# A GRU over 128 steps: both first rows of x on ScalarE's queue, r's input weights in two halves at the head of SyncE's, ten products of zeros ahead of the first real ones

## The chip, the core and the metric

The kernel runs on one core of a Trainium2 chip. A core has TensorE (PE, matrix products; its weight loads are listed as PEld), VectorE (DVE), ScalarE (ACT), GpSimd (POOL) and SyncE (SP), which only issues transfers here. Data come from HBM over DMA transfers, which an engine's instruction stream issues and 16 DMA engines carry out. Operands lie in on-chip memory of 128 partitions; TensorE writes to accumulator banks (PSUM), from which the vector engines read.

The metric is the time of one execution on the device in microseconds, as the median of several runs. Lower is better.

## The reference

`x` has 64 sequences of 128 steps with 512 values, `cond` the first state of 64 x 512. Each step of the GRU is

```python
comb = concatenate([x_t, h])
z = sigmoid(comb @ Wz + bz)
r = sigmoid(comb @ Wr + br)
h_cand = tanh(concatenate([x_t, r * h]) @ Wh + bh)
h_new = (1 - z) * h + z * h_cand
h_next = tanh(h_new @ Wp + bp)   # every 4th step but the last; otherwise h_new
```

and the result is `x` plus the sequence of `h_new`. All is float32. The upper 512 rows of Wz, Wr and Wh act on x, the lower 512 on the state.

## The kernel before, in words

**Two parts of each product.** The parts of the gates that come from x do not depend on the state. They are made ahead of the recurrence, as units in a queue that fill TensorE between the state's products (`put`, `fill`). For steps 0 to 3 they are plain products; from step 4 on, groups of steps share block products by a fast scheme on TensorE whose sums run on GpSimd and VectorE. The state's products (`gate`, four products of K for each of two halves of the batch) write to the tiles `rec_0`, `rec_1` and `rec_z`. The order of all instructions on each engine is the order in which the program writes them (`manual_schedule`); nothing reorders it.

**Names.** `wx` holds the weights for x of the three gates, `[128, K=4, 3, 512]`, 4 bytes a value: 1 MB for each gate, of which the four K parts are 256 KB each. `wh` holds those for the state. `x_rows` (L138) holds steps 0 and 1 of x as 64 rows of 512 each, 128 KB a step; `xT` the turned x. `scratch_q`, `_r`, `_a`, `_x`, `_y` are accumulator banks.

**The start, in the order of the program.**

1. VectorE sets the tile `zeros` (L67), GpSimd makes the identity matrix `ident`.
2. L140-141: the two rows of x are issued, step 0 over SyncE's queue (SP), step 1 over ScalarE's (ACT).
3. L142-143: r's weights for x are issued over SP in three pieces: K part 0, K part 1, and K parts 2 and 3 together (`load_wx`, L126 and L127).
4. L144-145: the biases over GpSimd's queue. L147: a dummy sigmoid on ScalarE, which loads its function table.
5. L149-152: z's and h's weights over SP, each in two halves of 512 KB; then step 2 of x (`load_step`, L122). L154: GpSimd copies one value of r's last K part, and by that waits for it; then it issues the two loads of the first state (L156).
6. L689: `idle(28)`, 28 products of zeros on TensorE (L236). Each has 512 columns of bf16 and one of four groups of 32 output partitions; four in a row go to the four groups, and they turn through `rec_0`, `rec_1` and `rec_z`. Nothing reads what they write.
7. L690-691: `turn_rows` turns the rows of steps 0 and 1, four transposes each on TensorE (L306) and one copy to `xT` each on VectorE (L311).
8. L692: `split_bias` on VectorE (L205-210). L693: `idle(4)`, four more products of zeros.
9. L694-696: r's products with x for steps 0 and 1 (L246), in the order of the pieces of the weights: for a piece, all its K parts of step 0, then of step 1. One K part of one step is 4 products, which the trace lists as 8 matmuls.
10. Then the loads of the state's weights over SP (L697-701), the first two K parts of z's products, the spreading of the biases (L217), the rest of z, h's products, step 2's and 3's, and from L720 on the first state and the recurrence.

SP's transfers share eight counters in turn. From the ninth on, a transfer is issued when the one eight places ahead of it has landed.

Of the kernel before, what the change touches and what calls it, by code (L numbers as in the profile page):

```python
# [18 lines left out]
def kernel(  # L19
# [14 lines left out]
    nc = tc.nc  # L34
    B, T, D = x.shape
# [7 lines left out]
    K = D // P  # L43
# [52 lines left out]
    def part(q):  # L96
        return slice(q * V, (q + 1) * V)
# [15 lines left out]
    both_queues = (nc.sync, nc.scalar)  # L113
# [12 lines left out]
    def load_wx(i, k0, k1):  # L126
        nc.sync.dma_start(  # L127
            out=wx[:, k0:k1, i, :],
            in_=gates_in[i][:D].rearrange("(p k) n -> p k n", k=K)[:, k0:k1],
        )  # L130
# [6 lines left out]
    x_rows = one.tile([P, Q4, S, J], F32, tag="xs0", name="x_rows")[:B].rearrange(  # L137
        "b t h u -> b (t h u)"  # L138
    )
    for t in range(2):  # L140
        both_queues[t].dma_start(out=x_rows[:, ts(t, D)], in_=x[:, t, :])  # L141
    for k0, k1 in ((0, 1), (1, 2), (2, K)):  # L142
        load_wx(R, k0, k1)
    for i, b in enumerate((br, bh, bz)):  # L144
        nc.gpsimd.dma_start(out=bias_in[:, i, :], in_=b.rearrange("(q j) -> q j", q=NQ))
# [9 lines left out]
    for h in range(S):  # L155
        nc.gpsimd.dma_start(  # L156
            out=h_rows[:, h, :],
            in_=h0[ts(h, V), :].rearrange("b (q j) -> q b j", q=NQ),
# [44 lines left out]
    def split_bias():  # L203
        high, low = thirds[:NQ], thirds[2 * V : 2 * V + NQ]
        nc.vector.tensor_copy(high, bias_in)  # L205
        nc.vector.tensor_sub(rest, bias_in, high)
        nc.vector.tensor_copy(middle, rest)
        nc.vector.tensor_copy(thirds[V : V + NQ], middle)
        nc.vector.tensor_sub(rest, rest, middle)
        nc.vector.tensor_copy(low, rest)  # L210
# [23 lines left out]
    def idle(n):  # L234
        for i in range(n):
            nc.tensor.matmul(  # L236
                rec[i // NQ % 3].rearrange("p a d n -> p (a d n)")[part(i % NQ)],
                lhsT=zeros[:, :V],
                rhs=zeros,
                start=True,  # L240
                stop=True,
            )
# [441 lines left out]
    def now(units):  # L684
        put(units)
        both(len(units))
# [3 lines left out]
    turn_rows(0, scratch[4])  # L690
    turn_rows(1, scratch[3])
    split_bias()  # L692
    idle(4)  # L693
    for part_k in (slice(0, 1), slice(1, 2), slice(2, K)):  # L694
        for t in range(2):
            now(first[R][t][part_k])
    load_wh(R)  # L697
# [373 lines left out]
```

## Time and profile before

| | |
|---|---|
| median of 3 runs | 1259.13 us (1259.06 to 1259.54) |
| the profiled execution's own time | 1258.66 us |
| its span, first to last instruction | 1256.6 us |
| TensorE busy | 1248.4 us |
| ScalarE, VectorE, GpSimd busy | 836.3, 809.1, 909.7 us |
| bytes moved, mean rate | 61.09 MB, 49 GB/s |

How to read the rows that follow. In an order of time, a row is: start in us from the span's start, length in us, engine, line, operation, out<-in, shape, count; in brackets the engine's idle time before it and what ended it. Like instructions in a row are merged. A "q" behind an engine's name (SPq, ACTq) means its instruction stream, which issues transfers. Matmuls are pipelined and their ends are modelled, so the distance from one start to the next tells more than the length. In a table of stretches, a row is: from:to, length, the busy time of PE, PEld, DVE, ACT and POOL with the number of instructions, the TensorE clock listed, the share of the 16 DMA engines and GB/s. In a DMA row, the last number is the time from issue to landing (the median, if there are several). In the list of waits: total, times, longest.

### The profile page before, as it was taken

The page shows a single profiled execution, that of the slowest core. Times are in us where ns is not written, and L with a number is a line of the kernel's source. Part 1 is how long each engine was busy: PE and PEld are TensorE (multiplying, and loading weights), DVE is VectorE, ACT ScalarE, POOL GpSimd, SP SyncE. Part 2 cuts the span into 40 slices and gives each one's busy share as a digit, 9 for nine tenths or more (in the row PEclk, how much of TensorE's full clock was granted, in tenths as well). Part 3 has the DMA queues.
Part 4 walks back from the last instruction along what each step waited for, and adds up shares of the span by engine and source line. Part 5 has one row for each costly group of instructions (what it writes and reads, how often), then busy time and mean ns, then how long its engine had stood idle before and what let it go on. Part 6 is the DMA issues. An engine that isn't in the chain of part 4 may idle for free.

```text
span 1256.6 us, 60732 instructions
## 1 busy us (share of the span) xinstructions
PE 1248.4 (99%) x25952; PEld 1155.6 (92%) x25952; DVE 809.1 (64%) x2183; ACT 836.3 (67%) x2687; POOL 909.7 (72%) x1032
## 2 busy tenths in 40 slices
PE   9999999999999999999999999999999999999998
PEld 5899999999999999999999999999999999999975
DVE  5666666666666666666666666666666666666554
ACT  2566666666666676666666666666676666666665
POOL 4988777777876788767777677787777787677530
PEclk9999999999999999999999999999999999999999
DMA  7311212121122120121111211111211112111011
GB/s 244 96 32 43 52 36 53 39 52 41 32 53 50 40 52 22 51 54 37 53 30 44 52 47 43 41 46 39 53 37 49 40 37 54 45 45 36 13 37 25
DMA packets 112290, 61.09 MB, mean 49 GB/s; under 512 B 12777, under 2 KB 109301, under 8 KB 112021
## 3 DMA queue, kind: packets, MB, share of 16 engines
q1 hardware_dynamic: 111588, 56.90, 17.0%
q8 instruction: 205, 3.36, 1.2%
q14 instruction: 65, 0.52, 0.1%
q0 software_dynamic: 256, 0.14, 0.1%
q10 hardware_dynamic: 176, 0.16, 0.1%
HBM read 40.38 MB, written 16.78 MB: 45 GB/s over the span
## 4 chain that ended last, share of the span: by engine, by line
PE 98%; DMA 1%; issue 1%; SPq 0%; DVE 0%; POOLq 0%; POOL 0%; ACT 0%; ACTq 0%
PE rec L246 45%; PE rec_z L246 16%; PE scratch_r L246 14%; PE scratch_q L246 11%; PE scratch_a L246 5%; PE scratch_y L246 4%; PE scratch_x L246 4%; DMA wx<-in_L_cond_Wr_dram 0%; SPq L886 0%; DMA out_dram<-xr 0%; SPq L127 0%; POOLq L1066 0%; POOL xr L876 0%; DVE z L980 0%; SPq L141 0%
## 5 line engine op out<-in xcount | busy, mean ns | idle before, releaser
L246 PE MATMUL rec<-wh,rhT 128*32 128x256 f32 x4096 | 376.6, 379 | 0.0
L246 PE MATMUL rec<-wh,hT 128*32 128x256 f32 x3072 | 282.9, 379 | 0.0
L246 PE MATMUL rec_z<-wh,hT 128*32 128x256 f32 x3072 | 282.8, 379 | 0.0
L246 PEld LDWEIGHTS rec<-wh,rhT 128*32 128x32 f32 x4096 | 248.5, 110 | 22.3 <-ACT rec L442 1.2
L281 ACT ACTIVATE scratch_r<-rec 64x128 f32<-64x128 f32 x512 | 128.0, 250 | 132.9 <-PE rec L246 65.3
L442 ACT COPY rec<-cp 64x256 f32<-64x256 f32 x512 | 189.9, 371 | 20.2 <-DVE cp L483 0.3
L246 PEld LDWEIGHTS rec<-wh,hT 128*32 128x32 f32 x3072 | 186.7, 110 | 16.2 <-issue 1.9
L246 PEld LDWEIGHTS rec_z<-wh,hT 128*32 128x32 f32 x3072 | 193.3, 110 | 8.1
L281 ACT ACTIVATE rec_z<-rec_z 64x128 f32<-64x128 f32 x488 | 122.0, 250 | 91.1 <-PE rec_z L246 79.2
L281 ACT ACTIVATE c<-rec 64x128 f32<-64x128 f32 x512 | 138.8, 271 | 60.7 <-PE rec L246 48.8
L876 POOL TENSOR_TENSOR xr<-xr,h 128x256 f32<-128x256 f32 x125 | 109.4, 876 | 85.3 <-DVE h L993 83.0
L621 POOL TENSOR_TENSOR cp<-mb,mb 128x768 f32<-128x768 f32 x76 | 139.2, 1831 | 9.3 <-DVE mb L587 5.7
L621 POOL TENSOR_TENSOR mb<-mb,mb 128x768 f32<-128x768 f32 x58 | 106.3, 1833 | 45.5 <-DVE mb L587 45.5
L621 POOL TENSOR_TENSOR cp<-mb 128x768 f32<-128x768 f32 x46 | 84.3, 1832 | 56.9 <-ACT rec_z L442 55.5
L246 PE MATMUL scratch_r<-tw,s 128*32 128x192 f32 x928 | 120.8, 326 | 0.0
L560 ACT COPY cq<-scratch_q 128x384 f32<-128x384 f32 x212 | 102.0, 481 | 19.2 <-PE scratch_q L246 17.7
L577 DVE TENSOR_TENSOR cx<-scratch_r,cx 128x384 f32<-128x384 f32 x106 | 59.1, 557 | 84.1 <-PE scratch_r L246 68.8
L246 PE MATMUL scratch_q<-tt,s 128*32 128x192 f32 x928 | 103.5, 326 | 0.0
L941 DVE SCALAR_TENSOR_TENSOR keep<-rec_z,h 128x256 f32<-128x256 f32 x91 | 38.6, 425 | 94.8 <-ACT rec_z L281 87.4
L583 DVE TENSOR_TENSOR mb<-scratch_q,cx 128x384 f32<-128x384 f32 x106 | 59.1, 558 | 62.4 <-ACT cq L560 62.4
L918 DVE TENSOR_TENSOR rh<-scratch_r,h 128x128 f32<-128x128 f32 x192 | 56.0, 292 | 61.2 <-ACT scratch_r L281 61.2
L246 PE MATMUL rec<-wp,hT 128*32 128x256 f32 x992 | 91.6, 379 | 0.1
(207 smaller groups left out, 3851.0 us busy)
## 6 DMA issues: line engine op xcount, KB each, us to landing
out_dram<-xr SPq DMA_DIRECT2D x249, 64.0 KB, 1.8
xr<-in_x_dram SPq DMA_DIRECT2D x248, 64.0 KB, 2.3
xs<-in_x_dram SPq DMA_DIRECT2D x240, 64.0 KB, 2.1
wx<-in_L_cond_Wz_dram SPq DMA_DIRECT2D x2, 512.0 KB, 7.8
wx<-in_L_cond_Wh_dram SPq DMA_DIRECT2D x2, 512.0 KB, 9.1
wh<-in_L_cond_Wr_dram SPq DMA_DIRECT2D x2, 512.0 KB, 7.7
wh<-in_L_cond_Wz_dram SPq DMA_DIRECT2D x2, 512.0 KB, 5.7
wh<-in_L_cond_Wh_dram SPq DMA_DIRECT2D x2, 512.0 KB, 9.4
```

What stands on the lines that cost most here:

```text
L246: nc.tensor.matmul(ps[part(2 * h + c)], lhsT=left, rhs=rhs(c), start=start, stop=True, skip_group_check=True,)
L281: nc.scalar.activation(o, v, func)
L442: nc.scalar.copy(gate_ps(i, h)[rows].rearrange("p d (c n) -> p d c n", c=C), G[t][rows, :, :, i, :].rearrange("p c d n -> p d c n"),)
L560: nc.scalar.copy(c[:, :nm], ps[:, :nm])
L577: nc.vector.tensor_add(T2[what][:, :nm], r_ps[:, :nm], T2[what][:, :nm])
L583: nc.vector.tensor_add(blocks(1, 1), runs(q_ps[:, :nm]), runs(T2[what][:, :nm]))
L621: nc.gpsimd.tensor_add(dst, a, b)
L876: nc.gpsimd.tensor_add(o, o, h_new.rearrange("p h (k e) -> p h e k", k=K))
L918: nc.vector.tensor_mul(rh[:, h, :], r_, h_old[:, h, :])
L941: nc.vector.scalar_tensor_tensor(out=kept[0], in0=kept[1], scalar=1.0, in1=kept[2], op0=ALU.subtract, op1=ALU.mult,)
```

## The change

Four lines in two places:

```diff
     for t in range(2):
-        both_queues[t].dma_start(out=x_rows[:, ts(t, D)], in_=x[:, t, :])
-    for k0, k1 in ((0, 1), (1, 2), (2, K)):
+        nc.scalar.dma_start(out=x_rows[:, ts(t, D)], in_=x[:, t, :])
+    for k0, k1 in ((0, 2), (2, K)):
         load_wx(R, k0, k1)
...
     split_bias()
-    idle(4)
-    for part_k in (slice(0, 1), slice(1, 2), slice(2, K)):
+    idle(10)
+    for part_k in (slice(0, 2), slice(2, K)):
         for t in range(2):
             now(first[R][t][part_k])
```

Both rows of x are issued by ScalarE, one behind the other. SyncE's first transfers are r's weights, in two pieces of 512 KB in place of 256, 256 and 512 KB. TensorE makes ten products of zeros between the turned rows and r's products, in place of four. r's products of K parts 0 and 1 are in one piece: both parts of step 0, then both of step 1, where they were part 0 of both steps and then part 1 of both. On VectorE and GpSimd the list of instructions is the same as before, and on ScalarE it is one issue longer; SyncE has two transfers fewer, one of x and one of r's weights. Each of SP's transfers from z's first half on still stands behind the same earlier transfers but for these.

## The prediction

> **What bounds the kernel now.** I read the page's totals and its chain first, then what TensorE waited for, then the order of time of the first 30 us, since every line of the diff lies there.
>
> ```profile
> PE 1248.4 (99%) x25952; PEld 1155.6 (92%) x25952; DVE 809.1 (64%) x2183; ACT 836.3 (67%) x2687; POOL 909.7 (72%) x1032
> PE 98%; DMA 1%; issue 1%; SPq 0%; DVE 0%; POOLq 0%; POOL 0%; ACT 0%; ACTq 0%
> ...
> PE rec L236 <- DVE zeros L67: 1.2, 1, 1.2
> PE scratch_q L246 <- DMA wx<-in_L_cond_Wr_dram: 1.1, 1, 1.1
> ```
>
> TensorE is busy for 1248.4 of 1256.6 us and makes up 98% of the chain. Its whole list of waits has two entries (the lower two rows): the 1.2 us until the zeros are set, and 1.1 us for r's weights. The diff does not touch the steps behind the start, so all that it can give back is this 1.1 us, or a little more if the products ahead of it start earlier. The order of time shows how the wait comes about (start, length, engine, line).
>
> ```profile
> 0.75 0.62 SPq L141 DMA_DIRECT2D x_rows<-in_x_dram  x1
> 0.76 0.58 ACTq L141 DMA_DIRECT2D x_rows<-in_x_dram  x1
> 1.20 1.04 PE L236 MATMUL rec<-zeros 128*32 128x512 bf16 x8 [1.20 <-DVE zeros L67]
> 1.43 1.84 SPq L127 DMA_DIRECT2D wx<-in_L_cond_Wr_dram  x3
> ...
> 3.31 0.64 PE L236 MATMUL rec_z<-zeros 128*32 128x512 bf16 x4
> 3.73 0.64 PE L236 MATMUL rec<-zeros 128*32 128x512 bf16 x4
> 4.30 0.74 PE L306 MATMUL scratch_y<-ident,x_rows 64*128 64x64 f32 x4
> 4.84 0.68 PE L306 MATMUL scratch_x<-ident,x_rows 64*128 64x64 f32 x4
> 5.45 0.62 PE L236 MATMUL rec<-zeros 128*32 128x512 bf16 x4
> 5.91 0.73 PE L246 MATMUL scratch_q<-wx,xT 128*32 128x256 f32 x8
> 6.45 0.62 PE L246 MATMUL scratch_a<-wx,xT 128*32 128x256 f32 x8
> 6.88 0.62 PE L246 MATMUL scratch_q<-wx,xT 128*32 128x256 f32 x8
> 7.32 0.62 PE L246 MATMUL scratch_a<-wx,xT 128*32 128x256 f32 x8
> 9.01 1.07 PE L246 MATMUL scratch_q<-wx,xT 128*32 128x256 f32 x16 [1.07 <-DMA wx<-in_L_cond_Wr_dram]
> 9.90 1.05 PE L246 MATMUL scratch_a<-wx,xT 128*32 128x256 f32 x16
> ```
>
> Lengths of matmuls overlap, so I count by the distance of their starts. The first half of r's products (four groups of 8) goes from 5.91 to about 7.75. The second half could follow at once, but starts at 9.01, when its weights have landed. The chain of waits names the issue behind it, and the DMA view the times to landing.
>
> ```profile
> 1.43 0.80 SPq L127
> ...
> 2.27 0.52 SPq L127
> ...
> 2.84 6.12 DMA wx<-in_L_cond_Wr_dram
> ...
> x_rows<-in_x_dram SPq DMA_DIRECT2D x1, 128.0 KB, 3.3
> x_rows<-in_x_dram ACTq DMA_DIRECT2D x1, 128.0 KB, 2.8
> ...
> wx<-in_L_cond_Wr_dram SPq DMA_DIRECT2D x2, 256.0 KB, 4.3
> ```
>
> SP issues the row of x at 0.75, then the three pieces of r's weights at 1.43, 2.27 and 2.84. They land near 5.7, 6.5 and 8.96. The rows of x land near 4.05 (SP) and 3.55 (ACT).
>
> **The change, part by part.**
>
> *The weights' place in SP's queue.* One issue goes (0.62 us, 0.68 to the next start), so r's weights are issued from 0.75 and not 1.43. A piece's issue goes too: the second half follows the first after 0.5 to 0.8 us (the 512 KB and 256 KB issues seen lie between), at 1.3 to 1.6 in place of 2.84. How much of that reaches the landing depends on the DMA engines:
>
> ```profile
> 2.50:3.00 0.50, 0.50 (x12) 0.23 (x8) 0.00 (x0) 0.35 (x2) 0.50 (x2) 1.00 1.03 345
> 3.00:3.50 0.50, 0.50 (x12) 0.20 (x8) 0.00 (x0) 0.00 (x0) 0.21 (x1) 1.00 0.50 100
> 3.50:4.00 0.50, 0.50 (x12) 0.00 (x0) 0.00 (x0) 0.00 (x0) 0.00 (x0) 1.00 0.52 145
> ...
> 6.00:9.00 3.00, 1.93 (x36) 0.91 (x32) 2.20 (x6) 0.00 (x0) 0.00 (x0) 1.00 0.92 309
> ```
>
> The last two columns are the DMA engines' share and GB/s. The rows of x move until 3.0; then there is a hole, 100 and 145 GB/s over 3.0 to 4.0, before the stream settles at 309. The hole is the time until SP's later issues take effect, so an earlier issue fills it. Two bounds for the landing of the second half: lower, the whole stream moves by the 0.68 us of issue and a bit (0.8): 8.96 - 0.8 = 8.15. Upper, all that is gained is that the 128 KB of one row no longer stand ahead in this queue: 128 KB at 309 GB/s are 0.42 us, so 8.55. I take the middle, **8.35**, since the hole shows the issue to matter and the second row of x still takes part of it. That is an estimate from these rows.
>
> *The rows of x on ScalarE's queue.* The first is issued at 0.76 as ACT's was, and lands near 3.6 to 3.9, before the first zeros end (3.73 + 0.42 = 4.15): the first transposes start at 4.2 to 4.3, as now. The second is issued one ACT issue (0.58) later, near 1.39. At 2.8 to 3.3 us it lands at 4.2 to 4.7, against the 4.6 at which the first four transposes are through; I take 4.5, and its transposes end as now or 0.2 later. Behind these two issues on ACT stand the table load and the dummy (1.37 to 2.86), 0.6 later; ACT's next work is at 12.93, which hides them.
>
> *Ten zeros for four.* Zeros go four at a time side by side, so ten are three rounds for one. Early rounds cost 0.42 (3.31 to 3.73). But the pace changes:
>
> ```profile
> 12.49 0.40 PE L217 MATMUL scratch_y<-thirds,picks 96*32 96x256 bf16 x8
> 12.71 0.29 PE L217 MATMUL scratch_a<-thirds,picks 96*32 96x128 bf16 x8
> ```
>
> Here eight bf16 products of 256 columns take 0.22 (12.49 to 12.71), the work of one round of zeros: half its 0.42. (The clock column lists 1.00 in the stretches above all the same, so I go by the pace.) The products say when it changed: the group at 5.91 takes 0.54 to the next, the later ones 0.43 and 0.44; at half pace a group would take 0.86, so 0.22 us of it ran slow, which puts the change at 6.13. Three rounds from 5.5 are then 0.63 slow (one and a half rounds) and 0.32 fast: they end at **6.45**. Bounds: all fast from 5.45, 6.1; all slow from 5.6, 6.9. Then r's first half, 1.73 at full pace (four groups of 0.43), ends at 8.2 (7.8 to 8.6). Its weights are there: even the second piece of now (2.27 + 4.3, near 6.5) comes no later with the stream moved up.
>
> *The sum.* The second half starts at the later of 8.2 and 8.35 and the 0.05 that 8.96 to 9.01 shows: 8.4, for 9.01. Gain **0.6 us**; by the ends of both bounds 0.3 to 0.9. The zeros and the later first half cost nothing, since their 0.5 us fall into what was the wait of 1.07. Against the earlier landing 0.2 of that cover is left; without it each tenth that the first half comes later is a tenth lost.
>
> *What is late next.* Behind r come the weights of z and h, x's third row, the turned state and h's weights.
>
> ```profile
> 10.49 0.43 DVE L362 TENSOR_TENSOR tt<-wx 128x256 f32<-128x256 f32 x1 [1.30 <-DMA wx<-in_L_cond_Wz_dram]
> 10.76 1.05 PE L246 MATMUL scratch_r<-wx,xT 128*32 128x256 f32 x16
> ...
> 16.61 0.67 DVE L297 STREAM_TRANSPOSE xT<-xr 128x256 f32<-128x256 f32 x1 [1.13 <-DMA xr<-in_x_dram]
> ...
> 18.00 3.64 PE L246 MATMUL scratch_q<-wx,xT 128*32 128x256 f32 x64
> ```
>
> z's first half has landed by 10.49 and is used at 10.76: 0.3 us of slack. x's third row is turned by 17.28 and used at 18.00: 0.7. If neither moved up, the first would cap the gain at 0.3. But z's weights stand in the same queue behind r's, with the same bytes ahead, so they move with r's; I cost this at nothing and keep 0.3 as an end. The next rows of x (L122) and h's weights are issued as earlier transfers land, so they move too. The POOL copy at L154 waits for r's last piece, and with it the two loads of h0 move up.
>
> So against the profiled execution's own 1258.66 (span 1256.6) I get 1258.06. That execution lay 0.47 below the median of the runs shown, 1259.13; for the median the forecast is **1258.5**.
>
> **The rivals.**
>
> *Hidden in the stream (no change).* r's weights, or z's behind them, come no earlier, because the same engines carry the same bytes: the gain is the 0 to 0.3 us of the caps above, 1258.8 to 1259.15. The 0.92 share from 6.0 to 9.0 speaks for it; the hole at 3.0 to 4.0 against it. [...]
>
> *The clock stays slow (at or a little above before).* The change to full pace comes when it comes, 4.9 us after the first zeros here (1.20 to 6.13). Were it to come at 8.0, the zeros would end at 6.78, 0.6 of the 1.73 us of products would be done by 8.0, and the second half would start at 9.1; before, its own first half would end at 8.7, still under 9.01. So the change would cost 0.1, 1259.2, and up to half a microsecond for a later one, 1259.6. Against it: the row at 5.91. [...]
>
> *The second row of x comes late (slower).* Its transfer now shares the engines with r's weights. From its landing the path is 0.23 to the transposes, 0.61 through them to the zeros, 0.64 of zeros at full pace and 1.73 of products: 3.2 us. It beats 9.01 only if it lands by 5.8, 4.4 us after its issue. r's own first piece took 4.3 today, so that point is within sight; 4.9 us would give 9.5, half a microsecond lost: 1259.6. Against it: alone in its queue but for the first row, it needs a quarter of the bytes of a half of r.
>
> **How the numbers follow.** Forecast 1258.5 (0.3 to 0.9 gained: 1258.2 to 1258.85): 0.58. Hidden: 0.18. Slow clock: 0.10. Late row: 0.10. Something not seen here: 0.04. The range takes in the forecast's bounds, the hidden case and most of the two slow ones, with the 0.3 us by which the median itself may lie elsewhere at the low end: 1257.9 to 1259.5. 0.2% of this kernel is 2.5 us, about what a measurement can tell from no change. No case above reaches it on either side: the whole wait is 1.1. So within 0.2%: 0.95; the 0.04 unseen I split, faster 0.02, slower 0.03 with the slow clock's far tail.
>
> **What would show it.** The wait of TensorE for r's weights shrinks to 0.1 to 0.4 us and the second half starts near 8.4; the first products start near 6.45 and not 5.91; the first bf16 rounds of the ten cost 0.42, the last about 0.22; the GB/s in 3.0 to 4.0 rise over 200; z's first products find their weights there. Wrong would be: zeros that start past 6.0 (late row), groups of products at 0.86 (clock), or a new wait for z's weights.

## The result, and the profile after

The changed kernel takes 1263.61 us (median of 6 runs, 1262.76 to 1264.67) against 1259.24 for the kernel before beside it: 4.4 us more, ratio 1.0035 with a 95% interval of 1.0025 to 1.0046. The forecast was 0.6 us less. The profiled execution took 1264.01 us, 5.35 over that of the kernel before.

The page of the changed kernel, its span and totals:

```profile
span 1261.8 us, 60743 instructions
...
PE 1251.0 (99%) x25958; PEld 1169.1 (93%) x25958; DVE 808.7 (64%) x2183; ACT 836.4 (66%) x2687; POOL 908.1 (72%) x1032
```

TensorE's waits in it:

```profile
PE scratch_y L306 <- DMA x_rows<-in_x_dram: 1.9, 1, 1.9
PE scratch_x L306 <- DMA x_rows<-in_x_dram: 1.7, 1, 1.7
PE rec L236 <- DVE zeros L67: 1.2, 1, 1.2
```

The wait for r's weights is gone, but only because r's products now start at 10.13, when both halves (5.3 and 7.65, see below) have long landed. In its place stand two waits for the rows of x, 3.6 us together. The order of time shows what follows from them:

```profile
3.73 0.64 PE L236 MATMUL rec<-zeros 128*32 128x512 bf16 x4
...
6.27 0.66 PE L306 MATMUL scratch_y<-ident,x_rows 64*128 64x64 f32 x4 [1.90 <-DMA x_rows<-in_x_dram]
...
8.63 0.74 PE L306 MATMUL scratch_x<-ident,x_rows 64*128 64x64 f32 x4 [1.70 <-DMA x_rows<-in_x_dram]
...
9.30 1.05 PE L236 MATMUL rec<-zeros 128*32 128x512 bf16 x8
...
10.13 2.33 PE L246 MATMUL scratch_q<-wx,xT 128*32 128x256 f32 x15
...
15.01 1.24 PE L246 MATMUL scratch_a<-wx,xT 128*32 128x256 f32 x14
...
15.87 1.24 PE L246 MATMUL scratch_r<-wx,xT 128*32 128x256 f32 x15
```

The second row's transposes start at 8.63, where they started at 4.84: 3.79 later. From there to r's first product it is 1.50 (8.63 to 10.13), where it was 1.07: 0.43 for the zeros. From r's first product to z's first (the row at 15.87) it is 5.74, where it was 4.85 with the wait for the weights in it: 0.89. The three make 5.11 of the 5.35 us, so nearly all of the loss lies ahead of z's products. At full pace (1.73 for a half, in the trace of the kernel before) r's products need 3.46 of the 5.74. Why they took 2.28 more is in the stretches, where the clock column (the third from the right) shows a change this time:

```profile
4.50:7.90 3.40, 0.66 (x4) 0.55 (x4) 0.42 (x1) 0.00 (x0) 0.22 (x2) 1.00 1.07 307
7.90:14.70 6.80, 6.07 (x56) 2.97 (x60) 4.97 (x13) 0.00 (x0) 1.33 (x2) 0.50 1.07 359
14.70:20.00 5.30, 5.30 (x110) 3.71 (x106) 2.16 (x7) 1.68 (x6) 0.00 (x0) 1.00 0.84 285
```

TensorE had full clock from 4.5 to 7.9, but did 0.66 us of work in it, waiting for the rows. Then it ran at half clock for 6.8 us, through all ten zeros and most of r's products.

Where the rows were shows in the DMA view by queue: q1 is SyncE's, q10 ScalarE's; packets, MB, share of 16 engines. The stretches are 1.7 to 3.75 (first row), 3.75 to 5.0 (next two), 5.0 to 5.75 (next two) and 5.75 to 7.0 (the two after). The last four rows are the issues with their times to landing.

```profile
q1 hardware_dynamic: 193, 0.40, 74.0%
...
q1 hardware_dynamic: 156, 0.29, 74.0%
q10 hardware_dynamic: 79, 0.13, 30.6%
...
q1 hardware_dynamic: 97, 0.20, 100.5%
q10 hardware_dynamic: 1, 0.00, 0.1%
...
q1 hardware_dynamic: 160, 0.29, 75.4%
q10 hardware_dynamic: 73, 0.12, 30.8%
...
wx<-in_L_cond_Wr_dram SPq DMA_DIRECT2D x1, 512.0 KB, 4.5
x_rows<-in_x_dram ACTq DMA_DIRECT2D x1, 128.0 KB, 5.4
...
wx<-in_L_cond_Wr_dram SPq DMA_DIRECT2D x1, 512.0 KB, 6.4
x_rows<-in_x_dram ACTq DMA_DIRECT2D x1, 128.0 KB, 7.3
```

Until 3.75 nothing at all moves on ScalarE's queue, though its first row was issued at 0.75, in the same moment as r's first half. The row (0.13 MB) moves when that half is nearly through; then the queue is silent again until the second half is nearly through. So the rows land at 0.75 + 5.4 = 6.15 and 1.33 + 7.3 = 8.6, each behind a half of r, which lands at 5.3 and 7.65.

### The profile page after: what moved, and what is told of

It reads as the page before. It is cut to its first block, busy times and chain, and to the rows that moved or that the text cites. A ratio compares the mean times of both kernels' runs of the same rounds, so it can differ in the third digit from the quotient of the medians.

```text
span 1261.8 us, 60743 instructions
## 1 busy us (share of the span) xinstructions
PE 1251.0 (99%) x25958; PEld 1169.1 (93%) x25958; DVE 808.7 (64%) x2183; ACT 836.4 (66%) x2687; POOL 908.1 (72%) x1032
## 4 chain that ended last, share of the span: by engine, by line
PE 99%; DMA 1%; DVE 0%; ACT 0%; ACTq 0%; issue 0%
PE rec L246 45%; PE rec_z L246 16%; PE scratch_r L246 14%; PE scratch_q L246 11%; PE scratch_a L246 5%; PE scratch_y L246 4%; PE scratch_x L246 4%; DMA x_rows<-in_x_dram 1%; PE rec L236 0%; DVE keep L941 0%; PE scratch_x L306 0%; DVE xr L983 0%; ACT z L281 0%; ACTq L141 0%; DVE xr L951 0%; DVE z L980 0%
```

## The experiments

**Theory.** The two queues take turns on the DMA engines by whole transfers, and the transfer whose issue ends first goes first. In the changed kernel r's first half is first (issued 0.76 to 1.21; the row 0.75 to 1.30), so the order is half, row, half, row. TensorE's wait for the rows then costs twice: by itself, and because the clock goes back to half. **Rivals:** the coarser pieces and the extra zeros cost the time; the queues share the engines evenly by bytes; ScalarE's queue is served later whatever it carries; the half clock costs nothing of its own.

*Rows on two queues again.* The changed kernel with

```diff
-        nc.scalar.dma_start(out=x_rows[:, ts(t, D)], in_=x[:, t, :])
+        both_queues[t].dma_start(out=x_rows[:, ts(t, D)], in_=x[:, t, :])
```

> The changed kernel with the rows of x back on two queues as before; r's weights in two halves and the ten zeros stay. Theory (the two queues take turns by whole transfers, so on ScalarE's queue each row of x waits for a half of r): the rows land near 4.0 us again, zeros end near 6.45, r's second half starts at 8.4 to 8.9, no half-pace stretch, 1258.6 to 1259.2 us. Rival (the coarser pieces and the extra zeros cost the time): still 1262 to 1264 us.

1259.06 us against 1258.68 before; ratio 1.0001 (0.9992 to 1.0011). With early rows the pieces and the zeros cost nothing that can be measured. The waits of TensorE in its trace, and z's first products:

```profile
PE rec L236 <- DVE zeros L67: 1.2, 1, 1.2
PE scratch_q L246 <- DMA wx<-in_L_cond_Wr_dram: 0.6, 1, 0.6
PE scratch_y L246 <- DMA wx<-in_L_cond_Wh_dram: 0.5, 1, 0.5
...
10.30 1.07 PE L246 MATMUL scratch_r<-wx,xT 128*32 128x256 f32 x16
```

z's products start at 10.30, 0.46 ahead of before, but then the second half of h's weights is late by 0.5: what is won at r is paid at h.

*The rows alone.* The kernel before, with only the first line of the change:

```diff
-        both_queues[t].dma_start(out=x_rows[:, ts(t, D)], in_=x[:, t, :])
+        nc.scalar.dma_start(out=x_rows[:, ts(t, D)], in_=x[:, t, :])
```

> The kernel before with only the two rows of x moved to ScalarE's queue; r's weights in three pieces of 256, 256 and 512 KB, four zeros. Turn theory: the first row starts when the first 256 KB are through, near 3.0 us, and lands near 4.8; the second behind the second 256 KB, near 6.2 (6.1 and 8.6 in the changed kernel). TensorE's idle time is about 2 us shorter than in the changed kernel; 1259 to 1260.5 us, by whether the pace stays full. Rival (the queues share the engines evenly by bytes, whatever the size of a transfer): the rows land as in the changed kernel, 6.1 and 8.6, and the time is 1262.5 to 1264 us. Rival (zeros and pieces cost it): as before, 1259.2 us, with the rows landing near 4.

1262.05 us against 1258.68; ratio 1.0022 (1.0013 to 1.0032): this line makes most of the loss, 3.4 of 4.4 us. With the rows late, the halves and the ten zeros together add the other 1.0; how they share it is not shown. The rows land after

```profile
DMA to landing us min/median/max: 5.0/5.6/6.3
```

5.0 and 6.3 us, at 5.75 and 7.6: earlier than behind halves of 512 KB (6.15 and 8.6), which speaks against even shares, but later than the 4.8 and 6.2 that I worked out. The reason is that the first 256 KB landed at 4.86 (0.76 + 4.1), only 0.4 ahead of the 512 KB in the changed kernel. Each row follows its piece by 0.8 to 1.0 in both: pieces at 4.86 and 6.82, rows at 5.75 and 7.6 here; halves at 5.3 and 7.65, rows at 6.15 and 8.6 there. The time is over what the theory gave; TensorE ran at half pace up to 12.9 in its trace.

*r in one transfer.* The changed kernel with `for k0, k1 in ((0, K),)` for the two pieces.

> The changed kernel with r's weights in one transfer of 1 MB. Turn theory: the first row waits for the whole 1 MB and lands at 7.5 to 8 us, the second for z's first 512 KB behind it, at 9 to 9.5; 1264 to 1266 us. Rival (even shares by bytes): the rows land no later than in the changed kernel, 6.1 and 8.6, and the time is the same, 1263.6 us.

1261.18 us against 1258.68; ratio 1.0021 (1.0012 to 1.0031). That is less than the changed kernel's loss, against the theory's 1264 to 1266, and the reason shows which transfer goes first. DMA view: 1.7 to 3.25, 3.25 to 5.25, 5.25 to 6.5 (two rows each).

```profile
q10 hardware_dynamic: 79, 0.13, 35.9%
q1 hardware_dynamic: 34, 0.07, 27.6%
...
q1 hardware_dynamic: 384, 0.79, 101.8%
q10 hardware_dynamic: 1, 0.00, 0.0%
...
q1 hardware_dynamic: 160, 0.30, 70.9%
q10 hardware_dynamic: 76, 0.13, 30.6%
```

The issue of 1 MB takes longer, 0.75 to 1.45, and ends behind the first row's (1.32). So the first row went first and landed at 3.7, and the second waited for the whole megabyte, to 7.6. I had taken the wrong transfer to be first; that the second row waits for a whole megabyte is what the rows show.

*The waits filled with zeros.* The changed kernel with

```diff
-    idle(28)
+    idle(60)
     turn_rows(0, scratch[4])
+    idle(36)
     turn_rows(1, scratch[3])
```

> The changed kernel with zeros that fill TensorE's waits for the rows: 60 in place of 28 ahead of the first row's transposes, and 36 between those and the second row's. Theory (of the loss, the half-pace stretch from 7.9 to 14.7 us makes a part of its own, because TensorE stood idle for the rows): no half-pace stretch after 6 us, rows as late as before, and 2 to 2.8 us less than the changed kernel: 1260.8 to 1261.6 us. Rival (the late rows alone make the loss): no change, 1263.6 us.

1261.71 us against 1258.68; ratio 1.0024 (1.0015 to 1.0034), just over the range expected. The rows are as late as in the changed kernel, but the stretch that ran at half clock there now reads

```profile
7.90:14.70 6.80, 6.80 (x124) 3.79 (x120) 4.67 (x12) 0.00 (x0) 1.37 (x2) 1.00 1.07 353
...
9.02 0.69 PE L306 MATMUL scratch_x<-ident,x_rows 64*128 64x64 f32 x4
...
13.54 1.24 PE L246 MATMUL scratch_r<-wx,xT 128*32 128x256 f32 x16
```

and z's products start at 13.54 in place of 15.87. The zeros overran a little: the second row landed at 8.6, its transposes start at 9.02.

The second set ran beside the changed kernel, whose own repetition comes first.

> The changed kernel once more, beside the others of this set on one chip. Both theories: 1263 to 1264.5 us, 4 to 5 us over the kernel before, the rows landing near 6.1 and 8.6 us.

1263.60 us against 1259.21; ratio 1.0035 (1.0022 to 1.0049), the rows at 6.2 and 8.6.

*The queues exchanged.* The rows head SyncE's queue, r's halves ScalarE's:

```diff
-        nc.scalar.dma_start(out=x_rows[:, ts(t, D)], in_=x[:, t, :])
+        nc.sync.dma_start(out=x_rows[:, ts(t, D)], in_=x[:, t, :])
     for k0, k1 in ((0, 2), (2, K)):
-        load_wx(R, k0, k1)
+        load_wx(R, k0, k1, nc.scalar)
```

> The changed kernel with the two queues exchanged: both rows of x head SyncE's queue, r's two halves head ScalarE's; z's and h's weights stay on SyncE's behind the rows. Theory (turns by whole transfers, and the transfer whose issue ends first goes first; 512 KB of r took 0.45 us to issue, a row 0.55 to 0.62): r's first half goes first, a row of x behind each half, which land near 6 and 8.5 us; 1262 to 1264 us. Rival (ScalarE's queue is served later, whatever it carries): the rows land near 4.1 and 4.8, r's halves late; 1259 to 1260.5 us.

1263.57 us; ratio 1.0035 (1.0023 to 1.0047). The rows land at 6.1 and 8.5, now over SyncE's queue:

```profile
wx<-in_L_cond_Wr_dram ACTq DMA_DIRECT2D x2, 512.0 KB, 5.4
x_rows<-in_x_dram SPq DMA_DIRECT2D x1, 128.0 KB, 5.3
```

Which queue it was made no difference here (6.15 and 8.6 in the changed kernel); r's first half ended its issue first again (1.18 against 1.36).

*Both rows in one transfer.* The changed kernel with

```diff
-    for t in range(2):
-        nc.scalar.dma_start(out=x_rows[:, ts(t, D)], in_=x[:, t, :])
+    nc.scalar.dma_start(out=x_rows[:, : 2 * D], in_=x[:, 0:2, :].rearrange("b t d -> b (t d)"))
```

> The changed kernel with both rows of x in one transfer of 256 KB on ScalarE's queue. Turn theory: it takes one turn behind r's first half and lands whole near 6.3 to 6.6 us, so the second row no longer waits for r's second half; the transposes of both rows run near 6.5 to 7.5, r's products from 8 to 8.5; 1259.6 to 1261.5 us, by how long the half pace lasts. Rival (a row is late in proportion to the bytes asked of ScalarE's queue): 256 KB land where the second row did, near 8.6; 1263 to 1264 us.

1262.66 us; ratio 1.0026 (1.0017 to 1.0036).

```profile
x_rows<-in_x_dram ACTq DMA_DIRECT2D x1, 256.0 KB, 6.5
```

Both rows land at 7.2, between the two theories: ahead of the second row's 8.6, and ahead of r's second half (8.26), so one turn, but later than the 6.3 to 6.6 forecast. The time is over the theory's range too; in its trace r's products ran at half pace until 13.7.

*Fewer zeros.* The kernel before with `idle(12)` for `idle(28)`.

> The kernel before with 12 zeros in place of 28 at its head, so that TensorE stands idle from 2.5 us until the rows come; no transfer moves. Theory (idle time early on costs by itself, since the pace goes up only after a stretch of work): rows and weights land as before, full pace only after 7.5 us or later, and 0.4 to 2.5 us more than before. Rival (pace does not matter, only the rows): no difference from before.

1259.20 us against 1259.21; ratio 1.0001 (0.9992 to 1.0010). The medians speak for the rival. In the profiled execution, 1260.17 us, r's first products did run at half pace:

```profile
6.61 1.07 PE L246 MATMUL scratch_q<-wx,xT 128*32 128x256 f32 x8
7.46 1.07 PE L246 MATMUL scratch_a<-wx,xT 128*32 128x256 f32 x8
8.32 1.07 PE L246 MATMUL scratch_q<-wx,xT 128*32 128x256 f32 x8
```

0.85 from group to group. Its z products start at 12.36, 1.60 later than before. Of this 0.70 was there at r's first product (6.61 for 5.91), since a row landed at 5.0 and not 4.05; the other 0.9 came with the half pace. Two other executions took 1258.7, and no trace shows their pace. So with early rows a late clock cost 0.9 us in one trace and nothing in the median; that the wait for r's weights, up to 9.0, covers much of it is argued, not shown.

The last set pits order against size. The changed kernel again:

> The changed kernel again, as the measure of the other three on one chip: 1263 to 1264.5 us, 4 to 5 us over the kernel before.

1263.38 us against 1259.32; ratio 1.0034 (1.0021 to 1.0046). And the kernel with the waits filled, beside it:

> The kernel with zeros in TensorE's waits once more, now beside the changed kernel: its part of the loss is that of the half pace. Theory: 1.2 to 2.4 us less than the changed kernel, 2.4 to 3.2 more than the kernel before (its products of z start 2.8 us later than before in the trace). Rival (the half pace costs nothing of its own): as the changed kernel.

1261.85 us; ratio 1.0023 (1.0014 to 1.0032): 1.5 us under the changed kernel, 2.5 over the kernel before. In its trace the zeros overran more: the second row's transposes start at 9.84, 1.2 behind the landing at 8.6.

*A small transfer ahead of r.* In both of the next two, one bias goes from GpSimd's queue to the head of SyncE's:

```diff
+    nc.sync.dma_start(out=bias_in[:, 0, :], in_=br.rearrange("(q j) -> q j", q=NQ))
     for k0, k1 in ((0, 2), (2, K)):
         load_wx(R, k0, k1)
-    for i, b in enumerate((br, bh, bz)):
+    for i, b in ((1, bh), (2, bz)):
         nc.gpsimd.dma_start(out=bias_in[:, i, :], in_=b.rearrange("(q j) -> q j", q=NQ))
```

> The changed kernel with one of the three 2 KB biases moved from GpSimd's queue to the head of SyncE's, so that r's first half is issued some 0.6 us later, behind the first row of x. Turn theory: the first row goes ahead of r's first half and lands at 3.6 to 4.2 us; the second, issued last of the three, still waits for that half, and lands at 6 to 6.6 in place of 8.6; 1260 to 1261.8 us. Rival (a row beside 512 KB on the other queue is late in any order): rows at 6 and 8.5, 1263 to 1264 us.

1261.13 us against 1259.32; ratio 1.0013 (1.0004 to 1.0022). r's first half is issued at 1.18, 0.4 and not 0.6 later, and the rows land at 4.5 and 7.0: each 1.6 earlier than in the changed kernel, by 2 KB put in front of 512. Both are later than the theory's 3.6 to 4.2 and 6 to 6.6; the time is in its range.

*The same, and both rows in one transfer.*

> As the kernel with one bias ahead of r's weights on SyncE's queue, and both rows of x in one transfer of 256 KB on ScalarE's. Turn theory: both rows go ahead of r's first half and land together at 4.2 to 4.9 us, r's halves near 6.3 and 8; TensorE works as in the kernel before: 1258.4 to 1259.6 us. Rival (late in any order): the rows land at 6 to 7.2, 1262 to 1263 us.

1259.57 us against 1259.32; ratio 1.0001 (0.9992 to 1.0010). Its issues, the queues from 1.7 to 3.0, and z's first products:

```profile
wx<-in_L_cond_Wr_dram SPq DMA_DIRECT2D x1, 512.0 KB, 5.0
x_rows<-in_x_dram ACTq DMA_DIRECT2D x1, 256.0 KB, 4.5
...
q10 hardware_dynamic: 41, 0.17, 64.7%
q1 hardware_dynamic: 7, 0.00, 0.5%
...
10.36 1.24 PE L246 MATMUL scratch_r<-wx,xT 128*32 128x256 f32 x16
```

The rows move first and land at 5.25, somewhat past the 4.2 to 4.9 expected; r follows and its second half lands at 7.6. The whole loss of 4.1 us in this set is gone, with both rows still on ScalarE's queue and r still in two halves. In its trace z's products start at 10.36, 0.4 ahead of before; in the medians nothing of that is left. No kernel here beats the one before.

## Why the prediction was wrong, point by point

- **The weights' place in SP's queue: right, and undersized.** Second half forecast at 8.35 (8.15 to 8.55), landed at 7.65, 0.5 ahead of the lower bound. This never came to use, since the products it was for were later still.
- **The rows of x on ScalarE's queue: the step that failed.** I put the first at 3.6 to 3.9 and the second at 4.2 to 4.7, from rows in which each queue carried one row and nothing large had been issued ahead of them. They landed at 6.15 and 8.6. I took the two queues to share the engines as the bytes come. A row instead waited for the whole of the large transfer whose issue ended ahead of its own: exchanged queues gave the same landings (6.1 and 8.5), smaller pieces earlier ones (5.75 and 7.6), and 2 KB ahead of r with one transfer for both rows (5.25) took the loss away. Whether the queues take turns, or all transfers stand in one line by the end of their issue, no run tells: in every trace the issues of the rows and of r's pieces end on the two queues alternately, so that both give the same order. What moved with nothing of a row in between is measured: 0.40 MB of r's first half from 1.7 to 3.75 (193 packets), and with r in one transfer 0.79 MB from 3.25 to 5.25 (384 packets, beside one of ScalarE's queue).
- **Ten zeros for four: the count was right, the pace wrong.** The rounds cost 0.4 each (8 in the row at 9.30 up to the last two at 10.13), with no fast one among them. With the rows on two queues again they were fast, 8 in 0.44 (5.38 to 5.82).
- **The late-row rival had the right outcome and break-even point.** It had the row late by sharing the engines, not by waiting for a whole half. It decided against the change from a landing of 5.8 on, and 3.2 us lie between landing and r's second half; 8.6 + 3.2 = 11.8 against 9.01 is 2.8 lost. With the waits filled, 2.5 and 3.0 were measured. Its sign, zeros that start past 6.0, came: they start at 9.30. But it got one chance in ten, and its counter-argument, "a quarter of the bytes", did not matter where a whole half went first. I had also argued that no case reaches 0.2%, because the whole wait is 1.1 us: that bounds what can be gained, not what a new wait can cost.
- **The clock rival was priced alone.** I gave it 0.1 to 0.5 us for a late change to full pace. Here a rise at 4.5 was taken back at 7.9, while TensorE, with 0.66 us of work in between, stood waiting for the rows: the first rival set off the second. Filling the waits with zeros gave 1.5 us back beside the changed kernel, 2.3 by the start of z's products in the two traces (15.87 against 13.54). So about 1.5 us or more of the 4.4 go to the half clock and at most the 2.5 to 3.0 that remain to the late rows, for part of what remains is the zeros' own overrun (0.4 and 1.2 us in the two traces). How much falls to the clock differs by execution. In three traces of the changed kernel full clock came for good at 14.7, 13.5 and 12.0 (the last two worked out from the pace of r's products: 16 matmuls in 1.71 before, in 0.86 after); z's products started at 15.87, 15.29 and 14.51, and the times were 1264.01, 1263.47 and 1262.70: half a microsecond for each microsecond by which the clock came later. No run shows the 8.0 for which I worked out the 0.1: with the rows on two queues again full pace was there at 5.38 (8 zeros in 0.44), and in the changed kernel it came for good at 12.0 to 14.7.
- **What is late next:** with early rows the gain of 0.4 to 0.5 at z did show, and was in one trace taken back by h's second half (0.5), not by z's, which I had named as the cap.

## What to carry to other kernels

When two queues carry loads at the start, a small transfer that the first work needs should end its issue ahead of any large one on the other queue. In these runs it otherwise waited for the whole of it: a row landed 5.4 us after its issue behind 512 KB and 6.2 behind 1 MB, against 2.8 to 4.2 with nothing large ahead. A large transfer at the head of its queue was not free just because its queue was another. A small transfer put ahead of the large one changed the order (1261.1 here), and joining the small ones into one saved a wait (1262.7); only the two together gave all of it back (1259.6). And price a wait of TensorE near the start with what it does to the clock (about 1.5 us here): rivals with one trigger add up.

## What the runs showed of the hardware that I had not expected

- Of two transfers issued together, the one whose issue ended first went first: 512 KB issued in 0.45 us went ahead of 128 KB issued in 0.55, and 1 MB issued in 0.70 behind it.
- Full clock was taken back where TensorE hardly used it: 4.5 to 7.9 full with 0.66 us of work, then 6.8 us at 0.50. With the queues exchanged it went the same way (the column averages 0.82 over 4.4 to 10.0 and 0.60 over 10.0 to 16.0). With r in one transfer TensorE had only the row's 0.69 us of transposes between the end of the zeros (4.33) and 7.64, and the column averages 0.78 over 4.4 to 10.0. In three traces it worked more from 4.5 to 7.9, and full pace, once it had come (8 zeros in 0.43 to 0.44), stayed: 2.51 us of work (small transfer ahead, both rows in one), 2.75 (rows on two queues), 3.32 (waits filled). What happens between these amounts of work no run shows.
- The clock column can read 1.00 at half pace. In the kernel with the rows alone it lists 1.00 from 7.7 to 12.9,

```profile
7.70:12.90 5.20, 5.20 (x48) 2.58 (x52) 3.69 (x10) 0.00 (x0) 1.55 (x3) 1.00 1.05 404
```

where 48 matmuls run in 5.2 us; at full pace, 8 in 0.43, they would take 2.6. The pace tells, not the column.
